# A two-layer graph kernel on one Trainium2 core: four more row blocks projected as pairs after the score vectors, and smaller moves

## The chip, the cores and the metric

The kernel runs on one core of one Trainium2 (trn2) chip. The metric is the time of one execution on the device in microseconds (us). A core has a tensor engine (TensorE, PE in the profile; its weight loads are listed apart as PEld), a vector engine (VectorE, DVE), a scalar engine (ScalarE, ACT), a general engine (GpSimd, POOL) and a sync engine (SyncE, SP) which issues plain transfers. Each has its own queue of instructions; they meet at semaphores.

## The reference, cut to what matters

x has 2708 rows of 1024 float32 numbers; adj is a 0/1 matrix of 2708 x 2708, sparse, with a few rows that have many neighbours.

```python
q = x @ W_q.T + b_q; k = x @ W_k.T + b_k; v = x @ W_v.T + b_v
z = (q @ k.T) / sqrt(1024) * adj
attn = softmax(where(z == 0, -10000, z), axis=1)
x = layernorm(x + relu(attn @ v))          # layer 0
x = layernorm(x + adj @ (x @ weight) + bias)   # layer 1
```

A row without neighbours has equal weights everywhere, so its attention is the mean of all rows.

## The kernel before, in words

The work is in `sparse_part` (from L81). A dense form stands behind a flag of the data and is not executed here.

**Layer 0.** Keys are never computed. M = Wq^T Wk is formed once (L609), and y = xM plus a constant is computed for every row (`y_block`, L288), so that the score of rows i and j is y_i times x_j. x comes transposed by `load_x` (L272, the transfer at L280) into three tiles xt in turn; a block of 128 rows is 16 products of 128x512 on PE (L319), two additions on DVE (L323), eight column sums of x on ACT (L332) and a store to the array y_d (L328). The last block has 20 rows: its tile is zeroed on POOL (L279), its products are 64 narrow ones (L305), and its sums go out in pieces. Behind it the column sums become the mean of x (L294, L295). The blocks of y go in file order, 0 to 21.

The rows are then taken in another order, by number of neighbours, in 22 blocks of records; `SLOTS` says how many neighbours each block has room for. The few largest rows are the "hub": their neighbours are dealt over 128 partitions, and the hub and block 0 (15 slots) are put together by `attend_shares` (L892). A block is worked on as follows. For each slot an indirect gather on POOL (L349) fetches neighbour rows of x into one of nine tiles g; DVE multiplies them with the row's y and sums (`score`, L792); a softmax is taken over pieces of at most six slots; DVE adds the weighted rows to r (L849, in `attend_shares` L926), of which `RB` = 3 tiles exist. The maximum of a piece is at L913. When the last piece of hub or block 0 is done, a generator entry waits in `joining` until two steps of the list have passed; then PE transposes the maxima (L934), DVE takes the joint maximum and weights (L936 to L940), and PE sums the denominators (L944).

Then r is multiplied by Wv. A block alone (step `("v", b)`): `flip` transposes r on PE (L716), or `flip_shares` does so for block 0 with products that also put the hub's rows in their place (L729); 16 products (L739); `finish0` (L879) adds the bias on DVE (L885, two halves), takes relu and adds x (L887), normalizes (`norm`, L767) and scatters to x1 (L703). The block of rows without neighbours is a step `("v", 21)`: `project_mean` (L745) with narrow products L752, a copy, and L761. Two blocks as a pair (step `("p", (a, b))`): both are transposed into rT tiles, DVE forms four sums of their halves (L965 to L968), and seven half products of four (28 instead of 32, L976, called from `pair_products` L990) with seven additions on DVE (L988) give both blocks; this needs four differences of weights, formed once (L1107 to L1110). `project_pair` (L1030) holds the tiles t, `finish_pair` (L1040) adds x (L1045), normalizes and scatters.

`norm` is a chain: the mean (L773, DVE), the sum of squares over 1024 elements (L775, ACT), a reciprocal square root through logarithm and exponential (ACT) with a correction step (DVE, up to L787), and the scaling of the 1024 elements (L788, ACT).

**What sets the order.** The list `steps` (L1060 to L1062) is written by hand: y blocks, among them single projections, then single projections, then seven pairs. Gathers, scores and sums are `jobs`, pulled in a loop (L1086 to L1142) by a credit of microseconds, and forced where a later step needs them; block 0's are forced from step 15 on (L1112). While y is unfinished one of the r tiles less may be held. At y of block 17 `row_constants(1)` (L1125) loads 13 blocks of x into g tiles from SP (L681) and forms one number for each row (L682). A scheduler then turns this program into the queue of each engine; additions that empty a bank of PSUM have a high priority. So the place of an instruction in its queue depends on the place of its step in the list, and on what it depends on.

**Layer 1** works on x1: `sum_rows` (L1197) gathers neighbours' rows of x1 and adds them (L1209, L1211); `gather_x1` (L1214) adds a row of its own to the bias; `turn1` and `work1` (L1235, `whole` at L1242) do transposes and pair products with the weights of layer 1 and their differences (L1264 to L1267); `finish1` (L1221) normalizes and scatters to the output. The units are one block (20) and ten pairs (L1192). The sums of units 0 and 1 are issued first, those of unit 2 at L1269 ahead of the loop, and within the loop (L1270) those of unit i + 3 during unit i.

Of the kernel before, what the change touches and what calls it, by code (L numbers as in the profile page):

```python
# [80 lines left out]
def sparse_part(ctx, tc, x, xT, adj, wqT, wkT, wvT, bq, bk, bv, w1, b1, out):  # L81
# [29 lines left out]
    with es:  # L111
# [159 lines left out]

        def load_x():  # L272
            b = len(xts)
            if b == NB:
                return
            r0, n = b * P, rows[b]
            xt = xa.tile([P, DC, P], F32, name="xt", bufs=3)
            if n < P:
                nc.gpsimd.memset(xt, 0.0)  # L279
            nc.sync.dma_start(out=xt[:, :, :n], in_=xT[:, r0:r0 + n].rearrange("(c p) n -> p c n", p=P))  # L280
            xts.append(xt)
# [48 lines left out]
        def column_sums(b, behind=None):  # L330
            for c in range(DC):
                put = nc.scalar.activation(junka, xts[b][:, c, :], AF.Copy, accum_out=xs[:, c, b:b + 1])  # L332
                if behind is not None and c % 2 == 0:
                    follow(put, behind[c // 2])
# [455 lines left out]

        def score(yg, xg, s, n):
            nc.vector.scalar_tensor_tensor(junkv[:n], yg[:n, :D], scale, xg[:n], op0=ALU.mult, op1=ALU.mult,  # L792
                                           accum_out=s)
# [85 lines left out]
        def finish0(b, po, xr):  # L879
            n = rows[b]  # L880
            t = wp.tile([P, D], F32, name="t")
# [10 lines left out]
        def attend_shares(b, got):  # L892
# [4 lines left out]
            else:  # L897
                J, tab, far_less, rec, to, far, top = J0, tab0, less0, tab0, to_0, far_0, top2[:, 1:2]
                r = wp.tile([P, D], F32, name="r", bufs=RB)
# [53 lines left out]

        def turn_pair(flips, pool):
# [13 lines left out]
            nc.vector.tensor_sub(S[3], a12, S[1])  # L968
# [61 lines left out]
        def project_pair(pair, A, S):  # L1030
            ts = [(xb_pools[0] if k else wp).tile([P, D], F32, name="t", bufs=2) for k in range(2)]
# [8 lines left out]
        def finish_pair(pair, ts):  # L1040
            for k, (b, t) in enumerate(zip(pair, ts)):
                xr, sums = pair_x[b], [stat.tile([P, 1], F32, name=f"sm{h}", bufs=6) for h in range(NH)]
                for h in (0, 1) if k == 0 else (1, 0):
                    th = halves_of(t)[h]
                    nc.vector.scalar_tensor_tensor(th, th, 0.0, halves_of(xr)[h], op0=ALU.max, op1=ALU.add, accum_out=sums[h])  # L1045
                norm(t, sums[0], P, sums[1])
# [9 lines left out]
        pairs = [(7, 20), (19, 18), (17, 8), (16, 11), (15, 10), (9, 14), (13, 12)]  # L1056
# [3 lines left out]
        steps = [("y", 8), ("y", 9), ("y", 10), ("y", 11), ("y", 12), ("v", 6), ("y", 13), ("v", 5), ("y", 14), ("v", 4), ("y", 15), ("v", 3),  # L1060
                 ("y", 16), ("v", 2), ("y", 17), ("y", 18), ("y", 19), ("y", 20), ("y", 21)]
        steps += [("v", b) for b in [1, 0] + last] + [("p", pair) for pair in pairs]  # L1062
# [27 lines left out]
        for i, (kind, b) in enumerate(steps):  # L1090
# [23 lines left out]
            while 0 in jobs and i >= 15:  # L1114
                credit -= run_job()
            while jobs and credit > 0 and len([c for c in got if c not in done0 and c not in ALONE and c != "hub"]) < (RB - 1 if left_y else RB):
# [3 lines left out]
            for k, c in steps[i:i + 2]:  # L1120
                if k != "y" and c not in turned and not (left_y and k == "p"):
                    turned[c] = turn0(c) if k == "v" else turn_pair([lambda rT, r=got[b_]: flip(r, rT) for b_ in c], xb_pools[0])
# [74 lines left out]
        def sum_rows(b, k=0):  # L1197
            if b == "hub":
                n, tab, ok, r = P, tab_h, valid_h, part
            else:  # L1200
                n, tab, ok = (P, tab0, valid0) if b == 0 else (rows[b], tabs[:, b, :SLOTS[b]], valid[:, b, :SLOTS[b]])
                r = (cp if k else wp).tile([P, D], F32, name="r", bufs=RB)
            for j in range(tab.shape[1] if b else J0):
# [4 lines left out]
                if j == 0:  # L1208
                    firsts.append(nc.vector.tensor_scalar(r[:n], xg[:n], ok[:n, 0:1], None, op0=ALU.mult))  # L1209
                else:  # L1210
                    nc.vector.scalar_tensor_tensor(r[:n], xg[:n], ok[:n, j:j + 1], r[:n], op0=ALU.mult, op1=ALU.add)  # L1211
# [9 lines left out]
        def finish1(b, t, sums):  # L1221
# [6 lines left out]
            norm(t, sums[0], n, sums[1])  # L1228
# [6 lines left out]
        def work1(unit, A, S, xrs):  # L1235
# [4 lines left out]
            def whole(k, h, acc, what):  # L1240
                with tc.high_priority(URGENT):
                    nc.vector.scalar_tensor_tensor(halves_of(ts[k])[h], acc, 1.0, what, op0=ALU.mult, op1=ALU.add,  # L1242
                                                   accum_out=sums[k][h])

# [24 lines left out]
        got1[2] = [sum_rows(b, k) for k, b in enumerate(units[2])]  # L1269
        for i, unit in enumerate(units):  # L1270
            for p in pending:
                finish1(*p)
            if i + 1 < len(units):
                turned1[i + 1] = turn1(units[i + 1], got1.pop(i + 1))
                xrs[i + 1] = [gather_x1(b, k) for k, b in enumerate(units[i + 1])]
            if i + 3 < len(units):
# [326 lines left out]
```

## Time and profile before

Three runs took 1083.0, 1079.15 and 1079.57 us, median 1079.57. The profile is of one execution of 1078.66 us; its span is 1076.9 us and its mean granted TensorE clock 0.984.

| engine | busy us | share | instructions |
|---|---|---|---|
| PE | 1007.8 | 94% | 2849 |
| PEld | 475.1 | 44% | 2849 |
| DVE | 847.2 | 79% | 1825 |
| ACT | 428.4 | 40% | 898 |
| POOL | 490.7 | 46% | 397 |

| group | count | busy us |
|---|---|---|
| L319 products of y | 672 | 292.2 |
| L976 products of pairs, both layers | 624 | 285.4 |
| L739 products of single blocks | 224 | 97.7 |
| L792 scores on DVE | 109 | 133.1 |
| L1211 sums of layer 1 on DVE | 77 | 98.6 |
| L849 weighted sums on DVE | 64 | 81.9 |

A 128x512 product of float32 stands as two records in the profile. Transfers moved 229.20 MB, 213 GB/s over the span. A line number is the line where the instruction is written, so a helper's line collects what all its callers do. The span is cut into 40 equal slices of 26.9 us in one view of the page, where a digit is the busy share of an engine in tenths. Others list, for a stretch of time that one names, each engine's busy time in it, or the instructions in order of time, with the idle time of the engine just before in brackets and what ended it.

### The profile page before, as it was taken

What the parts mean: (1) busy time and instruction counts of PE and PEld (TensorE: products, weight loads), DVE (VectorE), ACT (ScalarE), POOL (GpSimd) and SP (SyncE); (2) the same over time, 40 slices, a digit from 0 to 9 for tenths busy, and PEclk for the clock granted to TensorE, in tenths of its full rate; (3) what the DMA queues carried; (4) which work ended last, traced back from release to release, by engine and by line L of the source; (5) the groups of instructions that cost most, each with busy time, mean ns of one, the idle gap of its engine ahead of it and who ended that gap; (6) DMA issues with size and microseconds to landing.
All of it is one profiled execution on the core that took longest, in us unless ns stands there. A gap on an engine that the chain in (4) does not pass through costs nothing.

```text
span 1076.9 us, 10217 instructions
## 1 busy us (share of the span) xinstructions
PE 1007.8 (94%) x2849; PEld 475.1 (44%) x2849; DVE 847.2 (79%) x1825; ACT 428.4 (40%) x898; POOL 490.7 (46%) x397
## 2 busy tenths in 40 slices
PE   7999999999998999999997999899489999999993
PEld 6444444444443444444543444444244444454441
DVE  8799999994388889998497999874578777887431
ACT  4688698422132332224433344332422363333322
POOL 1000140057564536435246566611477777887300
PEclk9999999999999999999998999999899999999997
DMA  9555457564886756796422677735589589969601
GB/s 355 199 206 203 173 196 273 170 244 125 300 279 225 240 191 189 229 334 198 149 92 86 205 255 268 235 118 193 167 284 256 199 269 324 293 204 329 179 39 42
DMA packets 90963, 229.20 MB, mean 213 GB/s; under 512 B 18410, under 2 KB 40394, under 8 KB 88188
## 3 DMA queue, kind: packets, MB, share of 16 engines
q0 software_dynamic: 48768, 148.05, 43.0%
q1 hardware_dynamic: 42128, 80.41, 21.7%
q8 instruction: 24, 0.39, 0.1%
q14 instruction: 43, 0.35, 0.1%
HBM read 219.61 MB, written 33.68 MB: 235 GB/s over the span
## 4 chain that ended last, share of the span: by engine, by line
PE 18%; issue 12%; DVE 11%; DMA 4%; POOL 3%; ACT 2%; POOLq 0%; DVEq 0%; ACTq 0%
PE po L976 16%; DVE junkv L792 2%; DVE r L849 2%; DMA g<-x_d,tabs 2%; DVE r L1211 1%; DMA yg<-y_d,tabs 1%; ACT junks L775 1%; DVE t L988 1%; POOL xr L343 1%; PE tr L716 1%; POOL g L349 1%; POOL x_d L703 1%; PE po L739 1%; PE tr L729 1%; POOL r L349 1%
## 5 line engine op out<-in xcount | busy, mean ns | idle before, releaser
L319 PE MATMUL po<-m_sb,xt 128*128 128x512 f32 x672 | 292.2, 594 | 3.3 <-DVE yo L323 3.3
L319 PEld LDWEIGHTS po<-m_sb,xt 128*128 128x128 f32 x672 | 126.4, 190 | 159.6 <-issue 150.8
L792 DVE SCALAR_TENSOR_TENSOR junkv<-yg,g 128x1024 uint8<-128x1024 f32 x109 | 133.1, 1221 | 36.3 <-DMA yg<-y_d,tabs 16.6
L349 POOL DMA_INDIRECT g<-in_x_dram,tabs x86 | 115.9, 1347 | 76.1 <-DVE r L849 19.4
L976 PE MATMUL po<-t,s_all 128*128 128x512 f32 x272 | 125.5, 604 | 10.9 <-DVE t L988 6.6
L1211 DVE SCALAR_TENSOR_TENSOR r<-g,valid,r 128x1024 f32<-128x1024 f32 x77 | 98.6, 1281 | 18.1 <-DMA g<-x_d,tabs 17.2
L609 PE MATMUL po<-wk_o,wq_o 128*128 128x512 f32 x256 | 110.5, 592 | 0.0
L775 ACT ACTIVATE junks<-t,lnm 128x1024 uint8<-128x1024 f32 (+1 forms) x43 | 49.3, 1146 | 135.2 <-DVE lnm L773 104.7
L739 PE MATMUL po<-wv,rT 128*128 128x512 f32 x224 | 97.7, 594 | 3.3 <-DVE pr L834 2.8
L976 PE MATMUL po<-w,rT 128*128 128x512 f32 x192 | 87.8, 607 | 0.0
L976 PEld LDWEIGHTS po<-t,s_all 128*128 128x128 f32 x272 | 52.0, 194 | 78.4 <-issue 60.7
L563 POOL DMA_INDIRECT tab_d<-rec,pos_i x22 | 27.1, 1230 | 129.9 <-DVE pos_i L552 123.5
L849 DVE SCALAR_TENSOR_TENSOR r<-g,pr,r 128x1024 f32<-128x1024 f32 x64 | 81.9, 1279 | 5.5 <-ACT r L861 4.6
L349 POOL DMA_INDIRECT g<-x_d,tabs x67 | 75.0, 1120 | 22.7 <-issue 15.5
L332 ACT ACTIVATE junka<-xt 128x128 f32<-128x128 f32 x176 | 53.8, 306 | 72.0 <-PE po L319 55.5
L788 ACT ACTIVATE t<-t,nmr,rstd 128x1024 f32<-128x1024 f32 (+1 forms) x43 | 52.6, 1238 | 73.8 <-DVE nmr L787 73.7
L224 DVE MAX8 few<-a 128x8 f32<-128x75 f32 (+3 forms) x132 | 79.2, 618 | 0.0
L609 PEld LDWEIGHTS po<-wk_o,wq_o 128*128 128x128 f32 x256 | 48.4, 190 | 59.3 <-issue 59.0
L976 PE MATMUL po<-w,s_all 128*128 128x512 f32 x160 | 72.1, 592 | 0.0
L221 DVE SCALAR_TENSOR_TENSOR a<-a,iota 128x2708 f32<-128x2708 f32 (+1 forms) x22 | 65.2, 2963 | 5.4 <-ACT junk L220 5.4
L739 PEld LDWEIGHTS po<-wv,rT 128*128 128x128 f32 x224 | 42.3, 190 | 56.3 <-issue 55.2
L219 ACT ACTIVATE junk<-a 128x2708 uint8<-128x2708 f32 (+1 forms) x22 | 54.1, 2459 | 24.7 <-DMA a<-in_adj_dram 20.1
(339 smaller groups left out, 1503.3 us busy)
## 6 DMA issues: line engine op xcount, KB each, us to landing
a<-in_adj_dram SPq DMA_DIRECT2D x21, 1354.0 KB, 5.9
xt<-in_xT_dram SPq DMA_DIRECT2D x21, 512.0 KB, 4.8
y_d<-yo SPq DMA_DIRECT2D x21, 512.0 KB, 5.7
g<-in_x_dram SPq DMA_DIRECT2D x21, 512.0 KB, 7.7
wq_i<-in_wqT_dram SPq DMA_DIRECT2D x8, 512.0 KB, 9.3
wk_i<-in_wkT_dram SPq DMA_DIRECT2D x8, 512.0 KB, 10.4
wv<-in_wvT_dram SPq DMA_DIRECT2D x16, 256.0 KB, 6.0
w<-in_w_dram SPq DMA_DIRECT2D x4, 1024.0 KB, 7.6
```

The source lines that it names most:

```text
L219: nc.scalar.activation(junk[:n], a[:n], AF.Sign, accum_out=cnt[:n, b:b + 1])
L221: nc.vector.scalar_tensor_tensor(a[:n], a[:n], 1.0, iota[:n], op0=ALU.is_equal, op1=ALU.mult)
L224: nc.vector.max(few[:n, i * 8:(i + 1) * 8], a[:n, cuts[i]:cuts[i + 1]])
L319: put = nc.tensor.matmul(po, xt[:, c, :], m_sb[c // 2][:, c % 2, k0:k1], start=(c == 0), stop=(c == DC - 1))
L349: nc.gpsimd.indirect_dma_start(out=dst[:n], out_offset=None, in_=src, in_offset=bass.IndirectOffsetOnAxis(ap=at, axis=0), bounds_check=N - ...
L609: nc.tensor.matmul(po, wq_o[i // 2][:, o, i % 2 * P:(i % 2 + 1) * P], wk_o[:, o, hs], start=(o == 0), stop=(o == DC - 1))
L739: put = nc.tensor.matmul(acc, rT[:, c, :], w[c // 4][h][:, c % 4, :], start=(c == 0), stop=(c == DC - 1))
L775: nc.scalar.activation(junks[:n], t[:n], AF.Square, bias=nm[:n], accum_out=vs[:n])
L792: nc.vector.scalar_tensor_tensor(junkv[:n], yg[:n, :D], scale, xg[:n], op0=ALU.mult, op1=ALU.mult, accum_out=s)
L849: nc.vector.scalar_tensor_tensor(r[:n], xg[j][:n], pr[:n, j:j + 1], r[:n], op0=ALU.mult, op1=ALU.add)
L976: put = nc.tensor.matmul(acc, a[:, k], w[:, k], start=start and k == 0, stop=stop and k == DC // 2 - 1, skip_group_check=True)
L1211: nc.vector.scalar_tensor_tensor(r[:n], xg[:n], ok[:n, j:j + 1], r[:n], op0=ALU.mult, op1=ALU.add)
```

## The change

1. The single steps of blocks 3, 2, 1 and 0 are taken out of the list; two pairs, (3, 2) and (1, 0), are put at the head of the pairs, after the last y. Block 0's jobs are forced from step 12 of the shorter list on. Three r tiles may be held while y is unfinished, as afterwards. Within a pair block 0 is transposed by `flip_shares`. The mean's turned tile isn't made while y is unfinished.
2. Block 0's r lies in a tile of the group t instead of r. The t of block 0 and of the mean's block, and the second t of a pair, come from another pool with three tiles; before, the second t of a pair had two there.
3. x of the last 20 rows has a tile of its own, zeroed on DVE and loaded ahead of the first x; its column sums on ACT are as wide as the tile (32).
4. In layer 1 the sums of unit 2 are issued in the loop's first pass, behind the transposes and x1 gathers of unit 1, and their first DVE pass is kept behind the last of unit 1's half sums.
5. `norm_halves`: for the second block of the last pair, in both layers, the mean and variance come from batch-norm statistics of each half on DVE, taken as soon as that half is there, and the scaling is split between ACT and DVE.

```diff
@@ -271,2 +271,6 @@
 
+        xt_last = xa.tile([P, DC, HUB], F32, name="xt_last", bufs=1)
+        nc.vector.memset(xt_last, 0.0)
+        nc.sync.dma_start(out=xt_last[:, :, :rows[-1]], in_=xT[:, (NB - 1) * P:].rearrange("(c p) n -> p c n", p=P))
         def load_x():
@@ -276,5 +280,6 @@
             r0, n = b * P, rows[b]
+            if b == NB - 1:
+                xts.append(xt_last)
+                return
             xt = xa.tile([P, DC, P], F32, name="xt", bufs=3)
-            if n < P:
-                nc.gpsimd.memset(xt, 0.0)
             nc.sync.dma_start(out=xt[:, :, :n], in_=xT[:, r0:r0 + n].rearrange("(c p) n -> p c n", p=P))
@@ -331,3 +336,3 @@
             for c in range(DC):
-                put = nc.scalar.activation(junka, xts[b][:, c, :], AF.Copy, accum_out=xs[:, c, b:b + 1])
+                put = nc.scalar.activation(junka[:, :xts[b].shape[2]], xts[b][:, c, :], AF.Copy, accum_out=xs[:, c, b:b + 1])
                 if behind is not None and c % 2 == 0:
@@ -790,2 +795,23 @@
 
+        def norm_halves(t, stats):
+            mv = stat.tile([P, 2], F32, name="mv")
+            nc.vector.bn_aggr(out=mv, in_=stats.rearrange("p h e -> p (h e)"))
+            lv = stat.tile([P, 1], F32, name="lv")
+            nc.scalar.activation(lv, mv[:, 1:2], AF.Ln, bias=eps)
+            near = stat.tile([P, 1], F32, name="near")
+            nc.scalar.activation(near, lv, AF.Exp, scale=-0.5)
+            ve = stat.tile([P, 1], F32, name="ve")
+            nc.vector.scalar_tensor_tensor(ve, mv[:, 1:2], EPS, near, op0=ALU.add, op1=ALU.mult)
+            nc.vector.tensor_scalar(ve, ve, near, -0.5, op0=ALU.mult, op1=ALU.mult)
+            rstd = stat.tile([P, 1], F32, name="rstd")
+            nc.vector.scalar_tensor_tensor(rstd, ve, 1.5, near, op0=ALU.add, op1=ALU.mult)
+            nmr = stat.tile([P, 1], F32, name="nmr")
+            nc.vector.scalar_tensor_tensor(nmr, mv[:, 0:1], -1.0, rstd, op0=ALU.mult, op1=ALU.mult)
+            applied.append(nc.scalar.activation(t[:, :HALF], t[:, :HALF], AF.Identity, bias=nmr, scale=rstd))
+            nc.vector.tensor_scalar(t[:, HALF:], t[:, HALF:], rstd, nmr, op0=ALU.mult, op1=ALU.add)
+        def half_stats():
+            return stat.tile([P, NH, nc.vector.BN_STATS_DIM], F32, name="halves", bufs=2)
         def score(yg, xg, s, n):
@@ -880,3 +906,3 @@
             n = rows[b]
-            t = wp.tile([P, D], F32, name="t")
+            t = xb_pools[0].tile([P, D], F32, name="t", bufs=3) if b in [0] + last else wp.tile([P, D], F32, name="t")
             for h in range(NH):
@@ -898,3 +924,3 @@
                 J, tab, far_less, rec, to, far, top = J0, tab0, less0, tab0, to_0, far_0, top2[:, 1:2]
-                r = wp.tile([P, D], F32, name="r", bufs=RB)
+                r = wp.tile([P, D], F32, name="t")
             yg = wp.tile([P, YW], F32, name="yg")
@@ -953,2 +979,4 @@
 
+        halves_turned = []
         def turn_pair(flips, pool):
@@ -967,3 +995,3 @@
             nc.vector.tensor_sub(S[2], a11, a21)
-            nc.vector.tensor_sub(S[3], a12, S[1])
+            halves_turned.append(nc.vector.tensor_sub(S[3], a12, S[1]))
             return A, S
@@ -1030,3 +1058,3 @@
         def project_pair(pair, A, S):
-            ts = [(xb_pools[0] if k else wp).tile([P, D], F32, name="t", bufs=2) for k in range(2)]
+            ts = [(xb_pools[0] if k else wp).tile([P, D], F32, name="t", bufs=2 + k) for k in range(2)]
             bias = halves_of(bias_bc)
@@ -1041,2 +1069,3 @@
             for k, (b, t) in enumerate(zip(pair, ts)):
+                ends = half_stats() if k and pair == pairs[-1] else None
                 xr, sums = pair_x[b], [stat.tile([P, 1], F32, name=f"sm{h}", bufs=6) for h in range(NH)]
@@ -1045,3 +1074,8 @@
                     nc.vector.scalar_tensor_tensor(th, th, 0.0, halves_of(xr)[h], op0=ALU.max, op1=ALU.add, accum_out=sums[h])
-                norm(t, sums[0], P, sums[1])
+                    if ends is not None:
+                        nc.vector.bn_stats(out=ends[:, h, :], in_=th)
+                if ends is None:
+                    norm(t, sums[0], P, sums[1])
+                else:
+                    norm_halves(t, ends)
                 scatter(x1_d[:, :], b, P, t, "x1")
@@ -1055,3 +1089,3 @@
         jobs = [6, 5, 4, 3, 2, 2, 1, 1, "hub", "hub", 0, 0, 0]
-        pairs = [(7, 20), (19, 18), (17, 8), (16, 11), (15, 10), (9, 14), (13, 12)]
+        pairs = [(3, 2), (1, 0), (7, 20), (19, 18), (17, 8), (16, 11), (15, 10), (9, 14), (13, 12)]
         late_jobs = [7, 20, 8, 19, 18, 8, 17, 8, 16, 11, 15, 10, 20, 9, 14, 19, 13, 12, 18]
@@ -1059,5 +1093,5 @@
         jobs, late_jobs = jobs + late_jobs, len(late_jobs)
-        steps = [("y", 8), ("y", 9), ("y", 10), ("y", 11), ("y", 12), ("v", 6), ("y", 13), ("v", 5), ("y", 14), ("v", 4), ("y", 15), ("v", 3),
-                 ("y", 16), ("v", 2), ("y", 17), ("y", 18), ("y", 19), ("y", 20), ("y", 21)]
-        steps += [("v", b) for b in [1, 0] + last] + [("p", pair) for pair in pairs]
+        steps = [("y", 8), ("y", 9), ("y", 10), ("y", 11), ("y", 12), ("v", 6), ("y", 13), ("v", 5), ("y", 14), ("v", 4), ("y", 15),
+                 ("y", 16), ("y", 17), ("y", 18), ("y", 19), ("y", 20), ("y", 21)]
+        steps += [("v", b) for b in last] + [("p", pair) for pair in pairs]
 
@@ -1113,5 +1147,5 @@
                     credit -= run_job()
-            while 0 in jobs and i >= 15:
+            while 0 in jobs and i >= 12:
                 credit -= run_job()
-            while jobs and credit > 0 and len([c for c in got if c not in done0 and c not in ALONE and c != "hub"]) < (RB - 1 if left_y else RB):
+            while jobs and credit > 0 and len([c for c in got if c not in done0 and c not in ALONE and c != "hub"]) < RB:
                 if left_y and len(jobs) <= late_jobs:
@@ -1120,4 +1154,4 @@
             for k, c in steps[i:i + 2]:
-                if k != "y" and c not in turned and not (left_y and k == "p"):
-                    turned[c] = turn0(c) if k == "v" else turn_pair([lambda rT, r=got[b_]: flip(r, rT) for b_ in c], xb_pools[0])
+                if k != "y" and c not in turned and not (left_y and (k == "p" or c in last)):
+                    turned[c] = turn0(c) if k == "v" else turn_pair([lambda rT, b_=b_, r=got[b_]: flip(r, rT) if b_ else flip_shares([got["hub"], r], rT) for b_ in c], xb_pools[0])
                     done0.update(blocks_of((k, c)))
@@ -1196,3 +1230,3 @@
 
-        def sum_rows(b, k=0):
+        def sum_rows(b, k=0, behind=None):
             if b == "hub":
@@ -1201,3 +1235,3 @@
                 n, tab, ok = (P, tab0, valid0) if b == 0 else (rows[b], tabs[:, b, :SLOTS[b]], valid[:, b, :SLOTS[b]])
-                r = (cp if k else wp).tile([P, D], F32, name="r", bufs=RB)
+                r = (cp if k else wp).tile([P, D], F32, name="r", bufs=3 if k else RB)
             for j in range(tab.shape[1] if b else J0):
@@ -1208,5 +1242,9 @@
                 if j == 0:
-                    firsts.append(nc.vector.tensor_scalar(r[:n], xg[:n], ok[:n, 0:1], None, op0=ALU.mult))
+                    put = nc.vector.tensor_scalar(r[:n], xg[:n], ok[:n, 0:1], None, op0=ALU.mult)
+                    firsts.append(put)
                 else:
-                    nc.vector.scalar_tensor_tensor(r[:n], xg[:n], ok[:n, j:j + 1], r[:n], op0=ALU.mult, op1=ALU.add)
+                    put = nc.vector.scalar_tensor_tensor(r[:n], xg[:n], ok[:n, j:j + 1], r[:n], op0=ALU.mult, op1=ALU.add)
+                if behind is not None:
+                    follow(put, behind, same=True)
+                    behind = None
             return r
@@ -1227,3 +1265,6 @@
                     nc.scalar.activation(junks[:n, :HALF], halves_of(t)[h][:n], AF.Copy, accum_out=sums[h][:n])
-            norm(t, sums[0], n, sums[1])
+            if len(sums) == NH:
+                norm(t, sums[0], n, sums[1])
+            else:
+                norm_halves(t, sums[-1])
             scatter(out, b, n, t, "out")
@@ -1243,2 +1284,6 @@
                                                    accum_out=sums[k][h])
+                    if k and unit == units[-1]:
+                        if len(sums[k]) == NH:
+                            sums[k].append(half_stats())
+                        nc.vector.bn_stats(out=sums[k][-1][:, h, :], in_=halves_of(ts[k])[h])
 
@@ -1268,3 +1313,2 @@
         xrs = {0: [gather_x1(b, k) for k, b in enumerate(units[0])]}
-        got1[2] = [sum_rows(b, k) for k, b in enumerate(units[2])]
         for i, unit in enumerate(units):
@@ -1275,2 +1319,4 @@
                 xrs[i + 1] = [gather_x1(b, k) for k, b in enumerate(units[i + 1])]
+            if i == 0:
+                got1[2] = [sum_rows(b, k, halves_turned[-1]) for k, b in enumerate(units[2])]
             if i + 3 < len(units):
```

## The prediction, made before the changed kernel had run

> **What bounds the kernel now.** I read the page's slices first, then busy times by stage, then the instructions in order of time around each gap of TensorE (PE).
>
> ```profile
> PE   7999999999998999999997999899489999999993
> DVE  8799999994388889998497999874578777887431
> ```
>
> PE is the bound nearly everywhere: it dips in slice 22, in slice 29 and in the last one. VectorE (DVE) is as full as PE in slices 16 to 18, where the change works. The stages in numbers (span, then PE, weight loads, DVE, ScalarE (ACT), GpSimd (POOL), granted clock, DMA share, GB/s):
>
> ```profile
> 447.90:461.60 13.70, 13.70 (x33) 6.08 (x32) 13.70 (x26) 6.55 (x22) 4.08 (x4) 1.00 0.71 237
> 461.60:475.50 13.90, 13.90 (x35) 6.15 (x34) 13.67 (x23) 2.09 (x12) 1.41 (x2) 1.00 1.00 346
> ...
> 564.30:601.20 36.90, 30.30 (x78) 13.84 (x77) 28.80 (x55) 11.06 (x22) 23.06 (x12) 0.91 0.35 108
> 601.20:757.60 156.40, 151.84 (x407) 70.05 (x405) 128.91 (x309) 57.64 (x107) 71.56 (x57) 1.00 0.64 213
> 757.60:770.30 12.70, 0.24 (x4) 0.19 (x2) 3.24 (x11) 8.25 (x11) 4.38 (x5) 0.71 0.29 110
> ```
>
> From 448 to 475 us PE and DVE are both full: whatever leaves PE there finds DVE. The first pair (564 to 601) loses over 6 us; the seam between the layers leaves PE empty for 12.5. In order of time (start, length, instruction, idle before it):
>
> ```profile
> 497.15 0.15 DVE L913 TENSOR_TENSOR nm<-nm 128x1 f32<-128x1 f32 x1
> ...
> 512.42 3.67 PE L305 MATMUL po<-m_sb,xt 128*32 128x257 f32 x64 [1.29 <-DMA xt<-in_xT_dram]
> ...
> 583.37 1.29 DVE L988 TENSOR_TENSOR t<-po,bias_bc 128x512 f32<-128x512 f32 x2 [6.90 <-DMA x_d<-t,tabs]
> 584.12 6.08 PE L976 MATMUL po<-t,s_all 128*128 128x512 f32 x8 [6.60 <-DVE t L988]
> 592.61 3.60 PE L976 MATMUL po<-t,s_all 128*128 128x512 f32 x8
> ...
> 1059.82 1.15 ACT L775 ACTIVATE junks<-t,lnm 128x1024 uint8<-128x1024 f32 x1 [2.95 <-DVE lnm L773]
> 1062.49 1.24 ACT L788 ACTIVATE t<-t,nmr,rstd 128x1024 f32<-128x1024 f32 x1 [0.87 <-DVE nmr L787]
> 1064.00 0.95 POOL L703 DMA_INDIRECT out_dram<-t,tabs  x1 [5.91 <-ACT t L788]
> ```
>
> L913 is the third and last maximum of block 0's scores; PE takes it to its columns at L934 only at 503, so nothing waits. The last rows' x costs PE 1.29 us. The first pair waits 6.60 for a tile t whose old contents are still on their way out, and the eight passes after that take 6.08 instead of 3.60. A 128x512 product is two passes of 0.43, so 0.86. The last three lines are the norm that ends the kernel.
>
> **What the Trainium skill says.** "TensorE: Matmul & The Clock Gate", Part 1: PE runs at half its clock after an idle window of about 3.4 us. The trace agrees: 6.08 against 3.60 behind an idle of 6.60, none behind 1.29. Same page, Part 2: only weight loads are pulled ahead, matmuls stay in program order; so a transpose put early in PE's queue holds every product behind it. No line of before contradicts it. "DMA: Bandwidth & Descriptors", Issuing engines are not separate DMA queues: loads from SP and POOL share 16 engines; the stage at 461.60 shows them full (share 1.00). No page prices the batch-norm statistics.
>
> **The change, part by part.** The listing of the built instructions shows each engine's order unchanged up to block 15's sums in DVE's queue and, on PE, up to block 4's projection (ends 404.96).
>
> *Pairs.* Two blocks alone are 32 products, a pair 28: 8 x 0.86 = 6.9 us less PE work. Per pair DVE gets 4 sums, 7 additions and 4 half passes (15 x 0.61 = 9.2) for 4 additions and 2 full passes (4.8): 8.8 us more in all, beside PE's 24.
>
> *Behind y.* Blocks 3 and 2 leave the y stage, with them 2 x 13.74 of products and transposes (0.88 each). DVE's scoring of hub and block 0 stays. PE, now starting block 15 at 404.96, does four blocks (54.96), the hub's transpose (0.3) and two products (1.7), and is at 461.9. There the new order has L934 of block 0, two products into block 19 instead of behind it. What it waits for: before, DVE reached L913 at 497.15. Ahead of it go two finishes (2.9 each: additions 1.2, a pass 1.2, small ones 0.5), 12 passes of L682 (now behind it, 14.4), two scores of block 7 (2.4) and small operations (1.0); two additions of y come (1.2): 497.15 - 22.4 = 474.8. Its gathers are bounded by 0 (their waits of 2.3 are in that sum already) and about 4 us (twice as many x and y transfers fall into this stage): I take 1.1, 475.9. **A new wait of 14.0 us**, behind which stand the rest of y and everything else on PE, and a restart at half clock of 2.5 (6.08 - 3.60), bounded by 0 and 2.5.
> End of y: 475.9 + 0.3 + 14 products (12.0) + 9 (7.7) + L305 (3.7) + 7 (6.0) + 2.5 = 508.1, before 523.0. SP's 13 loads of x now stand ahead of two y stores; DVE frees their tiles by 492, the sums that need these stores come at 499.
>
> *From y to the first pair.* PE has nothing else here now. Eight column sums of the last rows on ACT (8 x 0.36), behind block 7's exponential, the mean's copy and the denominators: 4.2. Then the mean's L752 (3.7), transposes (0.5), blocks 3 and 2 (1.9), L761 (1.9), block 1 (0.9), L729 (3.5): 16.6, so 524.7. DVE's weight differences (4 x 2.2) start behind L752, at about 516, and are needed from 532 on: hidden.
>
> *Nine pairs.* 9 x 24.03 + 7 sets of two blocks' transposes (1.76) = 228.6, so 753.3. The first two pairs need no t that is in flight: block 0's sums hold one buffer only till L729, and the third buffer takes the mean; the 6.60 and its restart go. Late waits were 6.0 (156.4 less 150.4 of work). DVE's queue, added up from its rows, is ready 2 to 8 us ahead of each pair's transposes, least for 16 and 11 (100.6 us of DVE work behind the first pair's sums against 103.1 on PE). Bounds 0 and 6; I take 0.5: **753.8 against 757.6, -3.8**. A check by waits: -6.9 of products, -17.7 of old waits (1.3, 1.1, 9.1 and 0.2, 6.0), +21.2 of new ones (14.0, 2.5, 4.2, 0.5): -3.4.
>
> *Norms by halves*, once at the seam and once at the end, both on the path. Out go L773 (0.25), the squares (1.27) and half of L788 (0.57); in come the second half's statistics and their combination. Statistics of 512 elements appear in no row: the nearest is a DVE pass of that size, 0.61; bounds 0.5 and 1.2. I take 0.6, with 0.3 to combine: 2.1 - 0.9 = 1.2, less 0.1 for a handover: **-1.1 each, -2.2** (bounds -1.0 and -2.4). DVE's half (about 0.4, from 0.75 for 1024 at L1209) lies beside ACT's.
>
> *Third sums later.* Two x1 gathers (2.48 and 1.55 on POOL) now go ahead of the four of blocks 17 and 16. What ends PE's 2.99 us wait at 801.7 is DVE L988 behind sums of blocks 15 and 1, whose gathers stand behind the same number of transfers as before. Block 16's sum comes some 4 us later (was 787.5, its transposes started at 789.8): up to 2 us lost there and won at 801.7. Zero; bounds -3.5 and +2.
>
> *x early*: its 1.29 is counted; the zeroing moves from POOL to DVE, and the load is one of 80 KB among SP's first ones, where PE works on weights (190 us before its use): zero. The cp pool's three r buffers are three as before.
>
> Sum: -3.8 - 2.2 = -6.0 on a span of 1076.9, so 1070.9. Its run took 1078.66, the three runs shown 1079.15 to 1083.0, median 1079.57: **1073.6**.
>
> **Rivals.**
> *More is won (1065).* For it: the gathers' 1.1 may be nil and the restart too (PE gets one transpose, then work), the column sums may hide behind y's end (2), and the xr moved ahead may end the 3.5 at 801.7: -8.1 more, 1065.5. Against it: DVE is full from 448 to 503, so the 13 us stand.
> *The late waits stay (1079).* For it: they came from DVE reaching blocks' sums late, and DVE has 8.8 us more; with 6.0 instead of 0.5: 1079.1, no change.
> *DVE becomes the bound (slower, 1086).* One mechanism: gathers of block 0's pieces 2 and 3 and the 13 loads reuse nine tiles, each freed by the sum nine loads earlier, and the work that lay between is gone. The stage at 461.60 has the DMA engines full, and x and y transfers now come per 13.7 us, not 27. If each of these 23 loads makes DVE wait 0.6 us, DVE is 13.8 late; beyond the 1.8 or so of slack at 16 and 11 every microsecond reaches the end: +12.0, 1085.6. It decides from some 0.3 us per load on. Against it: a free tile came back loaded within 3.4 us from SP (468.2 to 471.6) and 5.9 from POOL (436.7 to 442.6), while the new order leaves 5 to 7.
>
> **How the numbers follow.** Forecast 0.50 (1069 to 1079, by the bounds above), more won 0.20, late waits stay 0.15, slower 0.15. What a measurement here can tell from no change is about 0.5%, 5.4 us: faster is below 1074.2, slower above 1085. Of the forecast's half, 0.28 lies below 1074.2, 0.22 above: faster 0.28 + 0.20 = 0.48, same 0.22 + 0.15 = 0.37, slower 0.15. The range goes to 1066 and 1085: about 0.05 is left out below, 0.12 above.
>
> **What would show it.** In the trace after: a wait of some 14 us on PE at L934 near 462 for DVE's maximum; y's end near 508 and the first pair near 525; no 6.6 us wait in the first pair; pairs of 24 us with hardly a gap up to 754; the scatter 1.1 us earlier behind the last product. The forecast is wrong if L934 doesn't wait (DVE's order or PE's is then not what I took), if DVE waits for gathers in many small pieces, or if the third sums change the 3 us at the second unit.

## The result, and the profile after

Four runs of the changed kernel took 1085.98 to 1090.24 us, median 1089.09, against 1079.86 of before: a ratio of 1.0075 (95% interval 1.0046 to 1.0105). It is slower by 9 us by the medians and 8 by the ratio; forecast was 6 us faster. The profiled run's span is 1088.0 us. Lines below are those of the changed kernel, where everything from `load_x` on stands lower: L305 became L310, L319 L324, L703 L708, L716 L721, L752 L757, L792 L818, L849 L875, L934 L960, L976 L1004, L988 L1016, L1045 L1074 and L1209 L1243. The maximum of a piece is L936 now; L939, which was L913, joins it with the maximum of the pieces before it.

The slices of the page, PE and DVE after:

```profile
PE   7999999999998999939999999999589999999993
DVE  8899999984587788898899889954578877896532
```

PE's dip is now in slice 18 (a 3), where before it was full; that of slice 22 (a 7) is gone, and the seam between the layers is still in slice 29, though a slice is 0.3 us longer now. In order of time, PE from the last y blocks to the seam (start, length, instruction, in brackets the idle time before it):

```profile
461.62 1.88 PE L324 MATMUL po<-m_sb,xt 128*128 128x512 f32 x4
480.06 0.45 PE L960 MATMUL tr<-ident,nm 128*128 128x128 f32 x1 [16.56 <-DVE nm L939]
480.30 22.28 PE L324 MATMUL po<-m_sb,xt 128*128 128x512 f32 x46
...
514.68 0.51 PE L190 MATMUL tr<-ident,xbT 128*128 128x128 f32 x3 [2.18 <-DVE tops L967]
...
515.45 5.35 PE L757 MATMUL po<-wv,mean 128*32 128x256 f32 x64
...
529.45 7.06 PE L1004 MATMUL po<-wv,rT 128*128 128x512 f32 x16
...
603.72 5.40 PE L1004 MATMUL po<-t,rT 128*128 128x512 f32 x8 [1.87 <-DVE t L1016]
...
628.80 3.70 PE L1004 MATMUL po<-wv,s_all 128*128 128x512 f32 x8 [0.69 <-DVE t L1016]
...
654.90 5.40 PE L1004 MATMUL po<-t,s_all 128*128 128x512 f32 x8 [3.46 <-DVE t L1016]
...
709.38 3.70 PE L1004 MATMUL po<-t,s_all 128*128 128x512 f32 x8 [0.72 <-DVE t L1016]
...
781.56 1.94 PE L721 MATMUL tr<-ident,r 128*128 128x128 f32 x8 [11.66 <-DVE r L1243]
```

The forecast wait at the transposed maximum is there, 16.6 us instead of 14.0. Unforecast are four waits inside pairs, 6.7 us together, each for an addition on DVE, two of them with a restart (5.40 instead of 3.60 for eight passes). Layer 0 ends its products at 769.6; before it was 757.6. What held the addition at 603 is seen on DVE:

```profile
597.06 1.28 DVE L875 SCALAR_TENSOR_TENSOR r<-g,pr,r 128x1024 f32<-128x1024 f32 x1
601.83 1.23 DVE L818 SCALAR_TENSOR_TENSOR junkv<-yg,g 128x1024 uint8<-128x1024 f32 x1 [3.49 <-DMA yg<-y_d,tabs]
602.98 0.08 DVE L818 DVE_READ_ACCUMULATOR junkv<-yg,g 128x1 f32 x1
602.98 0.68 DVE L1016 TENSOR_TENSOR t<-po,t 128x512 f32<-128x512 f32 x1
```

A score stands ahead of the addition in DVE's queue and waits 3.5 us for its row of y (tile yg). The Trainium skill ("TensorE: Matmul & The Clock Gate", table at the head) says that VectorE's queue is strictly first in, first out; this trace agrees: the addition that PE waits for goes only behind the score. DVE's waits from 530 to 720, by what ended them (total, times, longest):

```profile
DVE junkv L818 <- DMA yg<-y_d,tabs: 9.3, 3, 3.9
DVE t L1016 <- PE po L1004: 5.1, 5, 2.7
```

And the stages (span, then busy time of PE, weight loads, DVE, ACT, POOL, granted clock, DMA share, GB/s):

```profile
440.00:480.00 40.00, 23.50 (x56) 10.13 (x54) 36.04 (x56) 7.99 (x37) 16.19 (x12) 0.85 0.62 188
...
529.40:769.60 240.20, 233.46 (x618) 108.20 (x618) 196.45 (x445) 80.55 (x156) 115.13 (x84) 0.99 0.54 178
```

In the first DVE works 36 of 40 us while PE has 23.5; within PE's wait (463.50 to 480.06) DVE works 16.49 of 16.56 us. The tail after the last product: second half's addition, its statistics, their combination, the two halves of the scaling, the scatter.

```profile
1070.81 0.69 DVE L1283 SCALAR_TENSOR_TENSOR t<-po,xr 128x512 f32<-128x512 f32 x1 [1.43 <-PE po L1004]
...
1071.55 0.69 DVE L1288 BATCH_NORM_STATS2 halves<-t 128x6 f32<-128x512 f32 x1
1072.27 0.21 DVE L799 BATCH_NORM_AGGREGATE mv<-halves 128x2 f32<-128x12 f32 x1
...
1073.91 0.81 ACT L811 ACTIVATE t<-t,nmr,rstd 128x512 f32<-128x512 f32 x1 [0.86 <-DVE nmr L810]
...
1075.22 0.95 POOL L708 DMA_INDIRECT out_dram<-t,tabs  x1 [5.16 <-ACT t L811]
```

From the start of the last addition to the scatter it is 4.41 us, before 5.16 (1058.84 to 1064.00): 0.75 won.

### The profile page after: what moved, and what is told of

It reads as the page before. It is cut to its first block, busy times and chain, and to the rows that moved or that the text cites. A ratio compares the mean times of both kernels' runs of the same rounds, so it can differ in the third digit from the quotient of the medians.

```text
span 1088.0 us, 10191 instructions
## 1 busy us (share of the span) xinstructions
PE 1008.8 (93%) x2833; PEld 474.4 (44%) x2833; DVE 860.2 (79%) x1854; ACT 423.3 (39%) x894; POOL 491.4 (45%) x396
## 4 chain that ended last, share of the span: by engine, by line
DVE 35%; PE 23%; issue 18%; DMA 12%; POOL 9%; ACT 2%; POOLq 0%; DVEq 0%
PE po L1004 15%; DVE junkv L818 5%; DVE few L224 5%; DVE a L221 5%; DMA g<-in_x_dram,tabs 4%; POOL g L354 4%; DVE r L875 3%; DMA g<-x_d,tabs 3%; PE po L324 3%; DVE t L1016 2%; DMA yg<-y_d,tabs 2%; PE po L614 2%; DVE r L1246 2%; POOL tab_d L568 1%; DVE t L1074 1%
## 5 line engine op out<-in xcount | busy, mean ns | idle before, releaser
L324 PE MATMUL po<-m_sb,xt 128*128 128x512 f32 x672 | 294.2, 597 | 3.1 <-DVE yo L328 3.1
L324 PEld LDWEIGHTS po<-m_sb,xt 128*128 128x128 f32 x672 | 127.5, 192 | 161.7 <-issue 153.8
L818 DVE SCALAR_TENSOR_TENSOR junkv<-yg,g 128x1024 uint8<-128x1024 f32 x109 | 132.9, 1220 | 46.5 <-DMA yg<-y_d,tabs 20.9
L354 POOL DMA_INDIRECT g<-in_x_dram,tabs x86 | 112.6, 1309 | 89.6 <-DVE r L875 21.9
L1004 PE MATMUL po<-t,s_all 128*128 128x512 f32 x304 | 140.7, 606 | 7.8 <-DVE t L1016 4.2
L1004 PEld LDWEIGHTS po<-t,s_all 128*128 128x128 f32 x304 | 58.4, 194 | 84.8 <-issue 69.4
L780 ACT ACTIVATE junks<-t,lnm 128x1024 uint8<-128x1024 f32 (+1 forms) x41 | 47.0, 1147 | 104.0 <-DVE lnm L778 95.3
L1004 PE MATMUL po<-w,rT 128*128 128x512 f32 x192 | 86.4, 599 | 0.0
L875 DVE SCALAR_TENSOR_TENSOR r<-g,pr,r 128x1024 f32<-128x1024 f32 x64 | 81.7, 1279 | 0.9 <-ACT r L873 0.6
L337 ACT ACTIVATE junka<-xt 128x128 f32<-128x128 f32 x168 | 51.5, 306 | 77.4 <-PE po L324 58.7
L722 ACT COPY rT<-tr 128x512 f32<-128x512 f32 x80 | 43.2, 588 | 97.1 <-PE tr L721 97.1
L793 ACT ACTIVATE t<-t,nmr,rstd 128x1024 f32<-128x1024 f32 (+1 forms) x41 | 49.9, 1236 | 63.4 <-DVE nmr L792 63.1
L1004 PE MATMUL po<-w,s_all 128*128 128x512 f32 x160 | 72.1, 592 | 0.0
L1004 PE MATMUL po<-t,rT 128*128 128x512 f32 x152 | 70.1, 605 | 1.9 <-DVE t L1016 1.9
L1004 PE MATMUL po<-wv,s_all 128*128 128x512 f32 x144 | 64.8, 593 | 0.7 <-DVE t L1016 0.7
```

The source lines that it names most:

```text
L324: put = nc.tensor.matmul(po, xt[:, c, :], m_sb[c // 2][:, c % 2, k0:k1], start=(c == 0), stop=(c == DC - 1))
L337: put = nc.scalar.activation(junka[:, :xts[b].shape[2]], xts[b][:, c, :], AF.Copy, accum_out=xs[:, c, b:b + 1])
L354: nc.gpsimd.indirect_dma_start(out=dst[:n], out_offset=None, in_=src, in_offset=bass.IndirectOffsetOnAxis(ap=at, axis=0), bounds_check=N - ...
L780: nc.scalar.activation(junks[:n], t[:n], AF.Square, bias=nm[:n], accum_out=vs[:n])
L793: applied.append(nc.scalar.activation(t[:n], t[:n], AF.Identity, bias=nmr[:n], scale=rstd[:n]))
L875: nc.vector.scalar_tensor_tensor(r[:n], xg[j][:n], pr[:n, j:j + 1], r[:n], op0=ALU.mult, op1=ALU.add)
```

## The experiments

Each is compared with the kernel before, run on the same chip; chips differ (before took 1080 us in two groups of runs and 1093 in two others), so kernels of different groups are compared by their ratios. Lines in the views below are those of each run's own kernel.

### Which part costs

`pairs_only` is the kernel before with parts 1 and 2 of the change; `small_only` has parts 3, 4 and 5, with the four blocks left as single steps.

> Parts 1 and 2 of the change alone (four blocks as pairs behind y, block 0's r and the t tiles), on the kernel before. If the loss is theirs: the last product of layer 0 about 12 us later than before (it was 12.1 later in the changed kernel), the span 11 to 15 us longer, 1088 to 1094 us against 1080. If instead the small parts cost the time: within 3 us of before.

> Parts 3, 4 and 5 alone (x of the last rows early, third sums later, two norms by halves), with the four blocks where they were. If the loss lies in the pairs: 1076 to 1080 us, namely -0.75 for the last norm, about -0.8 for the seam, -1.3 for x, and 0 to +3 for the later third sums. If the small parts cost the time: above 1085 us.

Measured: pairs_only 1.0145 (1.0050 to 1.0241), small_only 0.9937 (0.9909 to 0.9965). So the loss is in the pairs' part, and the small parts gain some 4 to 10 us, at or above what was expected; the two together give the whole within their intervals.

### What of the pairs costs: two halves, and the t tiles

`one_pair` and `pair32` take the changed kernel and put one of the two pairs back as single steps.

```diff
# one_pair
-pairs = [(3, 2), (1, 0), (7, 20), ...
+pairs = [(1, 0), (7, 20), ...
-... ("v", 4), ("y", 15), ("y", 16), ("y", 17), ...
+... ("v", 4), ("y", 15), ("v", 3), ("y", 16), ("v", 2), ("y", 17), ...
-while 0 in jobs and i >= 12:
+while 0 in jobs and i >= 15:
-... < RB:
+... < (RB - 1 if left_y else RB):
# pair32
-pairs = [(3, 2), (1, 0), (7, 20), ...
+pairs = [(3, 2), (7, 20), ...
-steps += [("v", b) for b in last] + ...
+steps += [("v", b) for b in [1, 0] + last] + ...
```

> The changed kernel with blocks 3 and 2 back as single steps among the y blocks, so that only blocks 1 and 0 become a pair behind y; block 0's jobs forced from step 15 and two r tiles while y is unfinished, as before. If the y stage of the changed kernel lost because 27.5 us of PE work left it and VectorE's did not: no wait at the transposed maximum, y ends as before, the pair saves 3.4 us, and the wait of 6.6 with its restart 2.5 before the first pair's t goes: 6 to 14 us faster than before. If a pair behind y costs by itself (its sums and additions on VectorE, GpSimd's gathers): no faster than the kernel with the small parts alone, 0.3 to 0.6% below before.

> The other half of the pairs: blocks 3 and 2 as a pair behind y, blocks 1 and 0 as single steps. If the loss comes from PE work that leaves the y stage (VectorE full there): the wait of about 16 us at the transposed maximum is back as in the changed kernel, and the time is within 6 us of the changed kernel's, 7 to 10 us above before. If four blocks together were too many for the pairs' stage: like the one-pair kernel, 10 to 15 us below before.

Measured: one_pair 0.9853 (0.9831 to 0.9876), 1064.55 us; pair32 1.0081 (1.0052 to 1.0109), 1087.74 us. PE at the transposed maximum of pair32:

```profile
481.10 0.45 PE L960 MATMUL tr<-ident,nm 128*128 128x128 f32 x1 [16.71 <-DVE nm L939]
```

The wait is back in full. It comes with blocks 3 and 2 leaving the y stage. Three r tiles during y and the earlier forcing of block 0's jobs (step 12) stand in pair32 and were taken back in one_pair, so they go with the blocks here; no run took them apart. But is the gain of one_pair the pair's? `t3` has no new pair at all: the small parts, and from part 2 only the t tiles.

```diff
 # on small_only
-t = wp.tile([P, D], F32, name="t")
+t = xb_pools[0].tile([P, D], F32, name="t", bufs=3) if b in [0] + last else wp.tile([P, D], F32, name="t")
-... name="t", bufs=2) for k in range(2)]
+... name="t", bufs=2 + k) for k in range(2)]
```

> The kernel before with the small parts (x early, third sums later, norms by halves) and of the pairs' part only the t tiles: t of block 0 and of the mean from the other pool, three there; the four blocks stay single steps. The small parts alone gave a ratio of 0.9937 and kept the wait of 6.55 us at the first pair with its restart. If the t tiles are what the one-pair kernel owes most of its gain to: the wait and the restart go, up to 9 us less than the small parts alone, 1065 to 1070 us where before takes 1080. If the wait comes from elsewhere: no change against the small parts alone.

Measured: 0.9859 (0.9831 to 0.9886), 1064.74 us. All of one_pair's gain is in it. PE's waits in the pairs of t3 are five, of 0.15 to 1.26 us; the longest and the seam:

```profile
700.45 1.06 PE L721 MATMUL tr<-ident,r 128*128 128x128 f32 x8 [1.26 <-DVE r L875]
...
757.95 1.94 PE L721 MATMUL tr<-ident,r 128*128 128x128 f32 x8 [11.68 <-DVE r L1243]
```

The 6.6 us of before and its restart are gone. The pair (1, 0) saves 3.4 us of products, but the time shows no gain over t3: in one_pair PE has no single block to work on while ACT ends the last column sums, so it waits, and in the run profiled the mean's products then ran slowly (5.35 instead of 3.66 us in t3):

```profile
524.46 0.62 PE L190 MATMUL tr<-ident,xbT 128*128 128x128 f32 x4 [1.79 <-DVE xbT L300]
525.01 5.35 PE L757 MATMUL po<-wv,mean 128*32 128x256 f32 x64
```

The wait of 1.8 and the 1.7 by which the mean's products are longer make 3.5, as much as the pair saves. The 1.7 is not lost each time: `one_pair_third`, below, has the same wait and products of 3.66 us. Against t3, then, the four pairs cost 23.6 us at the end of layer 0 (its last products end at 746.0 in t3, 769.6 in the changed kernel); the t tiles and the small parts hid 11.6 of that (757.6 of before less 746.0).

### The wait in the y stage

`join3` moves block 0's transposed maximum later, `narrow` takes VectorE work away behind it (the thirteen passes for the row constants then leave out 960 of 1024 columns), `join3_narrow` does both.

```diff
# join3
-if i >= entry[1] + 2:
+if i >= entry[1] + (3 if entry[0] == 0 else 2):
# narrow
+w = D // 16 if f else D
-nc.vector.scalar_tensor_tensor(junkv, xg, 1.0, u_bc, ...
+nc.vector.scalar_tensor_tensor(junkv[:, :w], xg[:, :w], 1.0, u_bc[:, :w], ...
```

> The changed kernel, where block 0's transposed maximum (the wait of 16.6 us on PE) joins one step later, some 14 products later in PE's queue. Theory A, VectorE is the bound from 440 to 700 us and the wait is only where its lateness shows: the wait at the transpose falls by 12 us, the waits in the pairs grow by most of that, the end moves by less than 5 us (above 1084 us). Theory B, the place in the queue is what costs: waits in the pairs stay near 7 us and the time falls by 10 to 14 us, to 1075 to 1079.

> The changed kernel, where the thirteen passes for the row constants of blocks 8 to 20 read 64 of 1024 columns: their loads, their order and their waits stay, VectorE has about 13 x 1.1 = 14 us less between 478 and 505 us; the constants are wrong by what is left out. Theory A (VectorE is the bound): one pass of them lies ahead of the maximum, so the wait of 16.6 us shrinks by about 1 only, but the waits in the pairs (6.7 us with two restarts of 1.8) go for the most part: 8 to 12 us faster, 1077 to 1081. Theory C, the pairs' waits come from gathers that GpSimd issues late whatever VectorE does: under 3 us faster.

> Both edits together: block 0's transposed maximum one step later, and the thirteen passes of row constants on 64 columns (constants wrong by what is left out). With the later step alone the wait moved: 5.5 us at the transpose and 12.4 at the mean's transposes, for VectorE's L967. If VectorE's work in the y stage is what bounds it, the second wait falls to under 3 us and the first pair starts 10 to 14 us earlier, whatever follows; if something else holds L967, it stays near 12.

Measured: join3 1.0082 (1.0057 to 1.0108), narrow 1.0075 (1.0049 to 1.0102), join3_narrow 1.0041 (1.0027 to 1.0055). PE's waits of join3:

```profile
489.36 0.45 PE L960 MATMUL tr<-ident,nm 128*128 128x128 f32 x1 [5.53 <-DVE nm L939]
...
522.00 1.09 PE L190 MATMUL tr<-ident,xbT 128*128 128x128 f32 x4 [12.37 <-DVE tops L967]
```

5.5 and 12.4 are 17.9: the wait moved and nothing was won, which speaks against a mere matter of place. It did not move to the pairs, as theory A had it, but to the mean's transposes. Narrow failed theory A as it stood: DVE had 14 us less work behind the maximum, and neither the time nor the pairs' waits fell (9.1 us in all). That speaks against DVE's load as the cause of those waits, but not fully: DVE waited 8.1 of the 14 us for the thirteen loads into g tiles. In join3_narrow the second wait fell only to 9.1, not below 3, and DVE again stood waiting for these loads:

```profile
507.35 1.08 PE L190 MATMUL tr<-ident,xbT 128*128 128x128 f32 x4 [9.13 <-DVE tops L968]
```

```profile
DVE junkv L688 <- DMA g<-in_x_dram: 8.6, 7, 2.0
```

Behind DVE's passes stands a second limit nearly as long, the g tiles and their transfers. `score0` asked the same ahead of the maximum (block 0's scores then miss 960 of 1024 columns):

```diff
+w = D if b == "hub" else D // 16
-score(yg, xg[j], s[:, j:j + 1], P)
+nc.vector.scalar_tensor_tensor(junkv[:, :w], yg[:, :w], scale, xg[j][:, :w], ..., accum_out=s[:, j:j + 1])
```

> The changed kernel, where the fifteen scoring passes of block 0 read 64 of 1024 columns: gathers, order and waits stay, VectorE has 15 x 1.15 = 17 us less ahead of the last maximum; block 0's scores are wrong by what is left out. If VectorE's own work makes the wait of 16.6 us at the transposed maximum: it falls to 0 to 5. If the gathers and loads in front of those passes make it: it stays above 10. The pairs' waits (a third yg tile took them away) stay as they are; time 8 to 14 us below the changed kernel's in the first case, under 5 in the second.

Measured: 1.0055 (1.0032 to 1.0078), 0.2% below the changed kernel's ratio and within its interval. PE's wait, DVE's largest between 440 and 485 (total, times, longest), and a wait of GpSimd ahead of its gathers:

```profile
482.72 0.45 PE L962 MATMUL tr<-ident,nm 128*128 128x128 f32 x1 [10.72 <-DVE nm L941]
```

```profile
DVE junkv L934 <- DMA g<-in_x_dram,tab: 10.7, 6, 3.4
```

```profile
448.53 1.93 POOL L354 DMA_INDIRECT g<-in_x_dram,tab  x1 [5.97 <-DVE part L954]
```

With 17 us less of passes the wait fell by 6; DVE waits 10.7 us for gathers instead of 3.9. By the wait that remains and by the time this is the second case, though only just. But the gathers are late because of DVE in turn: a gather needs a g tile that a weighted sum has freed (GpSimd waits 5.97 us for the sums of L954 above), the sum needs the softmax of its piece, and the next scores need the gather. That ring kept 10.7 of the 16.6 us with its scoring passes short; its weighted sums were left at full width, so what they alone are worth was not measured.

### The waits in the pairs

`xr4` and `yg3` give the pairs' stage one more tile each, from the pool that replaces y's.

```diff
# yg3
-yg = wp.tile([P, YW], F32, name="yg")
+turn_y[0] += 1
+yg = xb_pools[0].tile([P, YW], F32, name="yg") if xb_pools and turn_y[0] % 3 == 0 else wp.tile([P, YW], F32, name="yg")
# xr4: the same for xr, every fourth
```

> The changed kernel with a fourth xr tile while the pairs run, so that GpSimd's gather of a pair's own rows waits less for VectorE's L1074 (25.6 us of GpSimd's waits between 535 and 735, with the gathers of y and x rows queued behind). Theory C (late gathers of y rows, head-of-line on GpSimd): VectorE's wait for yg, 9.3 us, falls below 4 and the time by 4 to 9 us. If the yg gathers are late for another reason (their own two tiles, transfer time): under 2 us.

> The changed kernel with a third yg tile while the pairs run. GpSimd waited 7.6 us between 535 and 735 for a free yg tile (VectorE L825 and L845). If that is what makes the y rows late: VectorE's wait for yg (9.3 us) falls below 4 and the time by 4 to 9 us; if the queue in front of it is: under 2 us.

Measured: xr4 1.0101 (1.0081 to 1.0122), no gain; yg3 1.0016 (1.0004 to 1.0027), on the same chip. DVE's wait for yg from 530 to 720 in yg3:

```profile
DVE junkv L821 <- DMA yg<-y_d,tabs: 2.8, 1, 2.8
```

```profile
606.83 3.70 PE L1007 MATMUL po<-t,rT 128*128 128x512 f32 x8 [1.27 <-DVE t L1019]
```

The line of PE is that of the wait at 603.7 above. 9.3 became 2.8, PE's waits in the pairs fell from 6.7 to 3.6 us in all, without a restart, and the ratio is 0.8% below that of xr4 in the same group and 0.6% below the changed kernel's, 6 to 9 us. From the last rows' products (L310) to layer 0's last product it is 260.5 us (506.2 to 766.7), in the changed kernel 267.1. In xr4 DVE's wait for yg stayed at 8.5. So having only two yg tiles made most of what is lost in the pairs. `score0_yg3` puts this and the narrow scores together:

> The same with a third yg tile in the pairs' stage. The two losses lie in two stages one after the other; if they are separate, their gains add: some 6 us below the kernel with the narrow scores alone, with which the four pairs would be at about 1068 to 1074, the forecast of the change. If one only hides the other, the sum is smaller.

Measured: 0.9994 (0.9967 to 1.0020), 0.6% below score0. So the third yg tile wins the same with the narrow scores as without. The narrow scores' own gain is 0.2% both times, which the intervals don't tell from nothing; that two gains add is therefore not shown. It did not reach the forecast: 10.9 us of the wait in the y stage remain.

### Two more on the best kernel

`one_pair_third` puts the third sums of layer 1 back ahead of the loop, `one_pair_yg3` has the third yg tile.

> The one-pair kernel with the third sums of layer 1 back ahead of the loop. The stretch from the first transposes of layer 1 to the last product was 288.5 us in the kernel before and 289.2 in the changed one. If the later third sums cost something: about 1 us less in that stretch than in the one-pair kernel; if they gain: 1 to 3 more.

> The one-pair kernel with a third yg tile while the pairs run. In the changed kernel the third tile took the pairs' waits away; in the one-pair kernel VectorE waits only 1.1 us for y rows, since PE comes to the pairs later against VectorE. Expected: within 2 us of the one-pair kernel. If it gains more than 3, the y rows held it back too.

Measured: 0.9857 (0.9828 to 0.9886) and 0.9838 (0.9798 to 0.9879), neither told apart from one_pair. Layer 1 from its first transposes to its last product took 288.2 us with the sums ahead of the loop and 289.8 later; before and after it was 288.5 and 289.2, in t3 (later) 288.6. If the later sums do anything, they cost up to 1.5 us. The versions at 1063 to 1065 us beat both kernels by 15 us or more; t3 is the simplest.

## Why the prediction was wrong

By its own steps:

- **Pairs, 6.9 us less PE work.** Right: PE has 16 records fewer (2833 instead of 2849), 6.9 us at 0.43 each.
- **The wait at L934**, 14.0, came as 16.6, with the restart of 2.5 (46 passes took 22.3 us, at 0.43 they are 19.8). It ended at 480.1 instead of 475.9: DVE waited 3.9 us for gathers there, and one pass of the row constants went ahead. y ended at 512.4 instead of 508.1. The mechanism was right and the size short; with the upper bound given for the gathers it would have ended at 478.8.
- **y to the first pair**, 16.6, took 17.0 (512.4 to 529.4). The column sums held PE up for less than 4.2, 2.2 us, and the mean's products took 1.7 longer than the 3.7 reckoned.
- **Nine pairs, late waits 0.5.** This step failed. The stage took 240.2 us, 11.1 more than the 229.1 forecast. DVE was indeed ahead of every pair's transposes, as worked out: PE waits at none of them. But the step considered only the transposes. Within a pair PE also needs each addition at once, and the additions stand in DVE's queue among scores that may wait for a transfer. The waits there are 6.7 us and the restarts 3.6; they account for 10.3. yg3 shows the cause of most of it, the two yg tiles: with a third, 6.6 of the 11.1 us went. The upper bound of 6 did not contain these waits either: it was the late waits of before, most of which are at transposes. That 6.0 was itself wrong: it takes the transposes of seven blocks in the stretch from 601.20, where nine stand; the line shown there has PE busy for 151.84 of 156.40 us, so the late waits were 4.6, and the check by waits gives -2.0 instead of -3.4.
- **No t in flight at the first pairs.** Right, and worth what was reckoned: t3 is 0.8% below small_only, some 8 us, for 9.1 of wait and restart. It was booked to the pairs, though they are not needed for it.
- **Norms by halves**, 1.1 each, gave 0.75 at the end and 0.8 at the seam (12.46 to 11.66; pairs_only, without them, keeps 12.45). The statistics take 0.69 for 512 elements, where 0.6 was taken, and ACT's half of the scaling 0.81, so that only 0.43 of its 1.24 is saved and not 0.57.
- **Third sums**, 0: right within 1 us (288.5 to 289.2), though the wait of 2.99 us at 801.7 became two, of 1.52 us and of 3.42 us with a restart. **x early**, 1.29: the wait is gone.

Together layer 0's last product came 15.8 us later than forecast (769.6 against 753.8): 4.3 were lost by y's end, 0.4 on the way to the first pair and 11.1 in the pairs.

The rival that ended slower named 1086 and VectorE. Its side was right, and that its size was near is luck: its 23 loads made DVE wait 3.9 us, not 13.8, all of it for gathers and none for the thirteen loads of row constants; and DVE's lateness did not reach PE at the pairs' transposes, where the rival put it, but at L960 and, by late rows of y, at the additions. In the rival with more won, the four gains named (1.1, 2.5, 2 and 3.5) make 9.1, not 8.1.

So 27.5 us of PE work left a stage that DVE and its ring of gathers could not shorten; the wait put 19 of them back, the pairs' own waits 10. What stays open is why two yg tiles are enough in t3 and one_pair and not with blocks 3 and 2 behind y (in pair32 DVE waits 6.5 us for yg, in t3 1.0); no run separated the order of GpSimd's queue from PE's earlier arrival.

## What to carry to other kernels

Before work is moved out of a stage, ask what the other engines there can do without it: PE's time in a stage is won only as far as their chain, buffers and transfers included, can be shortened too. Where one engine feeds another several times within a step, check every such handover, not only the first, and look for a waiting instruction ahead of it in the feeder's queue. A change of many parts can hide its best one: the t tiles, two lines, were worth nearly all that the best version won beyond the small parts.

## What was not expected of the hardware

PE's restart does not go by the length of the idle time alone. Behind idle times of 1.87 us (at 603.7) and 3.46 us eight passes took 5.40 us; behind 1.89 us in pair32 and 2.99 us in the kernel before they took 3.70:

```profile
814.16 3.70 PE L1004 MATMUL po<-t,s_all 128*128 128x512 f32 x8 [1.89 <-DVE xr L1016]
```

```profile
801.66 3.70 PE L976 MATMUL po<-t,s_all 128*128 128x512 f32 x8 [2.99 <-DVE xr L988]
```

Even the same wait at the same place can end either way: in one_pair_third PE waits 1.79 us ahead of the mean's products, as in one_pair, and they take 3.66 us instead of 5.35:

```profile
521.92 0.62 PE L190 MATMUL tr<-ident,xbT 128*128 128x128 f32 x4 [1.79 <-DVE xbT L300]
522.47 3.66 PE L757 MATMUL po<-wv,mean 128*32 128x256 f32 x64
```

The Trainium skill ("TensorE: Matmul & The Clock Gate", Part 1) gives an idle window of about 3.4 us and says that it runs freely and is not reset when a kernel starts. That equal idle times can end differently fits this, but no run here shows where the window lies. That 1.8 to 2.2 us can be enough does not fit a whole idle window, and here the measurement decides.
